# A two-stage attention kernel: the first slot of group 1 in an order of its own, three down-projections moved behind the slots of group 7

## The chip, the cores and the metric

The kernel runs on one NeuronCore of one Trainium2 chip. The metric is the device time of one launch in microseconds (us); less is better. A NeuronCore has engines that each take their own instructions in order: PE (TensorE, matrix products and transposes; PEld is its weight load), DVE (VectorE), ACT (ScalarE), POOL (GpSimd) and SP (SyncE, here the queue of most transfers). They meet through semaphores: an instruction waits until the instructions that it needs have counted up.

## What is computed

The reference has two stages. Stage one is a graph attention over 64 graphs of 64 nodes and 256 features; stage two is a transformer block with a conditioning vector per graph.

```python
# stage one: x is (64, 64, 256), q a vector per graph, adj a label array
self_feat = concat(x, q) @ W_self.T + b_self
output = self_feat
for d in range(2):                     # adjacency and its transpose
    cond, vb = A.sum(-1), A @ w_bias + b_bias
    aff = q_heads . k_heads * scale    # keys: the first 20 nodes alone
    w = softmax(where(cond > 0, aff, NEG) + vb)
    output += (w @ self_feat[:, :20]) @ Wout[d] + bout[d]
x = x + relu(output)
# stage two, per graph: shift, scale, gate from silu(time_emb) @ Wt + bt
h = layernorm(x) * (1 + scale_msa) + shift_msa
x = x + gate_msa * (attention(h) @ Wproj + bproj)     # 16 heads of 16
h = layernorm(x) * (1 + scale_mlp) + shift_mlp
x = x + gate_mlp * (gelu(h @ W1 + b1) @ W2 + b2)      # MLP of 1024
```

All of it is float32.

## The kernel before

**Groups and tiles.** The 64 graphs are cut into nine groups: 4 graphs, seven times 8, and 4 again. A tile (index j) is two graphs, 128 tokens; group 0 and group 8 have two tiles, the others four. Features lie on the partitions for the projections; the attention works on 128 tokens at a time.

**A software pipeline over groups, written out by hand.** The order of the program is the order on every engine's queue. `start()` does the graph stage of groups 0 and 1. Then, for g from 1 to 7, `boundary(g)` prepares projections, layer norms and masks, and `period(g)` runs the slots of group g. `finish()` ends groups 6 (its MLP), 7 and 8. In period(g) three things run side by side: the block attention of group g (E), the graph attention of group g+1 (C), and the MLP of group g-1. Each slot j takes one tile of each.

**A slot** (`slot`, L763) goes through these steps, and at named points (`fill("f0")`, `"f1"`, `"d0"`, ...) it inserts the work that a table in `period` (L976 to L1023) lists:

1. PE: scores of E and of C (L618, L458).
2. Transposes of the tile before, `block_turned(Eb)` (L654), copied to pT by ACT (L657). In the first slot of a period there is no tile before. Then f0.
3. POOL: masked keys for the next slot (L603, L441).
4. `block_exp(E)`: two maxima (L629) and two subtractions (L631) on DVE, an exponential on ACT (L635).
5. `graph_masked(C)`: two products on DVE (L469) and a sum on POOL (L474). Then f1.
6. `graph_turned` of the tile before (PE L496, ACT copies wT L500), if there is one.
7. `block_sums(E)`: a sum over keys on DVE (L639). Then d0.
8. `graph_exp(C)`: maximum (L479) and subtraction (L480) on DVE, exponential on ACT (L481). Then d0b.
9. `block_weights(E)`: a reciprocal on DVE (L642) and POOL's product (L643) that writes the normalised weights pr. The next slot's `block_turned` needs them.
10. Attention products of the tile before: pao (PE L665, ACT aoT L675), po (PE L514, DVE L523, ACT L524, POOL L525).
11. `graph_normal(C)`: sum and reciprocal on DVE (L486, L487), product on POOL (L488). Then d2 and f3.

**Fills that matter here.** `mlp_up` (L735) is a product on PE followed by a gelu on ACT (L737); `mlp_down(m, c, i)` (L745) adds block i of 8 to the output half c; a call of the 512-column form is two matmuls. `mlp_gated` (L680, DVE) reads the sum and gives its PSUM bank back, `mlp_out` adds on POOL (L758) and issues the output transfer on SP. `block_v` (L588) is a product on PE and four copies on ACT (L595). `self_cond` for group 3 is one product on POOL (L315) per half; `self_product` and `self_features` are pf on PE (L324) and an addition on DVE (L331). `half_normed` is the layer norm of the next group in four steps: transposes (L533), statistics (L542 to L546), normalising (L551), transposes back with scale and shift (L560, L563, L567). ACT has to load a table (ACT_TABLE_LOAD) between an exponential and a gelu; copies and biases need none.

**PSUM.** Most products take a bank from a ring of four (`free`); `mlp_down` holds one from its first block until `mlp_gated`, so that three go round. A product waits until the last reader of its bank is done.

**The two places.** In group 1's first slot the table puts `block_v(1, 1)` and the two `self_cond` of group 3 (`conds`) at f1, and four `mlp_up` at f3. In period 7, only three slots are run from the table, and the last tile's scores (E3) stand in `finish`; the table gives slot 2 `down(0, 2, 3)` at f0 and `down(0, 4, 5)` at f1, and `finish` goes on with 6 and 7:

```python
        E3 = block_scores(m, 3, [pair("pa", "sca"), pair("pb", "scb")])
        block_turned(before[0])
        half_normed(z, 2)
        mlp_down(l, 0, 6, 7)
        block_attended(before[0], bank("pao"))
        block_exp(E3)
```

Of the kernel before, what the change touches and what calls it, by code (L numbers as in the profile page):

```python
# [26 lines left out]
NG = len(NB)  # L27
# [19 lines left out]
def graph_attention_then_dit_block(  # L47
# [576 lines left out]
    def block_exp(t):  # L624
        mx = small.tile([P, 2, 2, 4], F32, tag="mx1", name="mx1")
        t.pr = two.tile([P, H, N], F32, tag="pr", name="pr")
        pa4 = [p_.rearrange("p q (h m) -> p q h m", m=N) for p_ in t.pa]
        for i in range(2):
            nc.vector.tensor_reduce(mx[:, i], pa4[i], AX.X, ALU.max)  # L629
        for i in range(2):  # L630
            nc.vector.tensor_tensor(  # L631
                t.pr[:, ts(i, 8)].rearrange("p (q h) m -> p q h m", q=2), pa4[i],
                mx[:, i].unsqueeze(3).to_broadcast([P, 2, 4, N]), ALU.subtract,
            )
        nc.scalar.activation(t.pr, t.pr, AF.Exp)  # L635

    def block_sums(t):
        t.sm = small.tile([P, H], F32, tag="sm1", name="sm1")
        nc.vector.tensor_reduce(t.sm, t.pr, AX.X, ALU.add)  # L639
# [5 lines left out]
    def block_normal(t):  # L645
        block_sums(t)
        block_weights(t)
# [91 lines left out]
    def mlp_down(g, c, *ms):  # L739
        G = groups[g]  # L740
        for m in ms:
            if m == 0:
                py, G.held = bank("py", hold=True)
                G.py = py[:, 0 : G.T]
            nc.tensor.matmul(G.py, w2_sb[:, m, ts(c, P)], G.u[m], start=(m == 0), stop=(m == 7))  # L745

    def mlp_gated(g, c):
        G = groups[g]
        if c == 0:
            y = gp.tile([P, 2, GT], F32, tag="h2T", name="y2T")  # L750
            G.y2T = [y[:, i, 0 : G.T] for i in range(2)]
        gated(G.y2T[c], G.py, "b2", 1, g, c)
        free.append(G.held)
# [6 lines left out]

    def slot(e, c, e_next, c_next, before, fill, late=False):  # L763
        Eb, Cb = before
        fill("p")
        sc = [pair("pa", "sca"), pair("pb", "scb")] if e or c else None
        E = block_scores(*e, sc) if e else None
        C = graph_scores(*c, sc) if c else None
        fill("p2")
        if Eb:  # L770
            block_turned(Eb)
        elif Cb:
            graph_turned(Cb[0])
        fill("f0")
        if e_next:
            block_keys(*e_next)
        if c_next and c_next[0] != 1:
            graph_keys(*c_next)
        if E:
            block_exp(E)  # L780
        if c_next and c_next[0] == 1:
            graph_keys(*c_next)
        if C:
            graph_masked(C)
        fill("f1")
        if Eb and Cb:
            graph_turned(Cb[0])
        if E:
            block_sums(E)
        fill("d0")  # L790
        if C and not late:
            graph_exp(C)
        fill("d0b")
        if E and not late:

            block_weights(E)
        if Eb:
            block_attended(Eb, pair("pa", "pao")[:, 0])
        fill("f2")
        for i, t in enumerate(Cb):  # L800
            if i > 0:
                graph_turned(t)
                fill("f2a")
            graph_output(t, pair("pa" if i > 0 else "pb", "po")[:, 0])
        if late:
            graph_exp(C)
            block_weights(E)
        fill("f2b")
        fill("d1")
        if C:  # L810
            graph_normal(C)
        fill("d2")
        fill("f3")
        return E, [C] if C else []
# [115 lines left out]
    def half_normed(g, step):  # L930

        G = groups[g]
        if step == 0:
            norm_tokens(G, G.xT, 0)
        elif step == 1:
            norm_stats(G)
        elif step == 2:
            normed(G)
        else:
            G.hT = new_hT("hT")  # L940
            modulated(G, G.hT, 0, amp1, off1, g)

    def run_slots(slots, fills, before):

        for i, (e, c) in enumerate(slots[: len(fills)]):

            def fill(where):
                for f, *args in fills[i].get(where, []):
                    f(*args)

            e_next, c_next = slots[i + 1] if i + 1 < len(slots) else (None, None)
            before = slot(e, c, e_next, c_next, before, fill, fills[i].get("late", False))
        return before

    def period(g):

        m, n, a = g - 1, g + 1, g + 2
        late = g + 2 >= NG

        def up(*ms):  # L960
            return [(mlp_up, m, i) for i in ms]

        def down(c, *ms):
            return [(mlp_down, m, c) + ms] if not late or c == 0 else []

        def masks(*steps):
            return [(mask_step, a, i) for i in steps] if a < NG else []

        def ahead(f, *args):
            return [(f, a) + args] if a < NG else []  # L970

        def next_(f, *args):
            return [(f, n) + args] if n < NG else []

        G = groups[g]
        gated_0 = [(mlp_gated, m, 0), (mlp_out, m, 0)]  # L976
        conds = ahead(self_cond, 0) + ahead(self_cond, 1)
        if G.nt == 2:
            fills = [
                {  # L980
                    "f0": up(0),
                    "f1": [(block_v, g, 0)] + up(1, 2),
                    "f3": up(3, 4, 5) + down(0, 0, 1, 2),
                },
                {
                    "f0": down(0, 3) + up(6),
                    "f1": up(7),
                    "f2": down(0, 4, 5),
                    "f3": down(0, 6, 7) + gated_0,
                },  # L990
            ]
        else:
            fills = [
                {
                    "f1": [(block_v, g, i) for i in range(1 if g in (1, NG - 2) else 0, 2)] + (conds if g == 1 else []),
                    "d0": masks(0) if g > 1 else [],
                    "d2": masks(1) + conds if g > 1 else [],
                    "f3": up(0, 1, 2, 3),
                },
                {  # L1000
                    "f0": down(0, 0, 1),
                    "f1": ahead(self_product, 0),
                    "d0": ahead(self_features, 0),
                    "f2b": ahead(self_product, 1),
                    "d1": ahead(self_features, 1),
                    "d2": masks(2, 3) if g > 1 else masks(0),
                    "f3": up(4, 5),
                },
                {
                    "f0": down(0, 2, 3),  # L1010
                    "f1": down(0, 4, 5),
                    "f2": ahead(graph_v, 0),
                    "d2": masks(3) if g == 1 else [],
                    "f3": up(6, 7),
                },
                {
                    "f0": next_(half_normed, 0) + down(0, 6),
                    "f1": down(0, 7) + gated_0 + next_(half_normed, 1),
                    "f2": down(1, 0, 1, 2),
                    "d0b": next_(half_normed, 2),  # L1020
                    "f3": down(1, 3, 4, 5, 6) + next_(half_normed, 3) + down(1, 7),
                },
            ]  # L1023
        if n == NG - 1:

            fills = fills[:3]
            fills[1].update(f0=down(0, 0), f2=down(0, 1))
            fills[2]["f3"] = up(6) + next_(half_normed, 0) + [(pair_proj, g, 0)] + up(7) + next_(half_normed, 1)
        C = groups[n].nt if n < NG else 0
        slots = [((g, j), (n, j) if j < C else None) for j in range(G.nt)]  # L1030
        return run_slots(slots, fills, (None, []))
# [117 lines left out]
    def finish(before):  # L1149

        z, m, l = NG - 1, NG - 2, NG - 3
        Z, A = groups[z], groups[m]
        K = [Tile() for _ in range(3)]
# [1 line left out]
        E3 = block_scores(m, 3, [pair("pa", "sca"), pair("pb", "scb")])  # L1155
        block_turned(before[0])
        half_normed(z, 2)
        mlp_down(l, 0, 6, 7)
        block_attended(before[0], bank("pao"))
        block_exp(E3)  # L1160
        mlp_gated(l, 0)
        mlp_out(l, 0)
        half_normed(z, 3)
        norm_tokens(K[0], A.xT, 0)
        mlp_down(l, 1, 0)
        block_normal(E3)
        norm_stats(K[0])
        mlp_down(l, 1, 1)
        mlp_down(l, 1, 2)
        block_qk(z, 1, 0)  # L1170
        block_qk(z, 1, 1)
        block_keys(z, 0)
        block_turned(E3)
        block_qk(z, 0, 0)
        block_qk(z, 0, 1)
# [70 lines left out]
    before = start()  # L1246
    for g in range(1, NG - 1):
        boundary(g, before)
        before = period(g)
# [60 lines left out]
```

## Time and profile before

| what | us |
|---|---|
| median of 3 runs | 675.4 (675.13 to 675.85) |
| the profiled execution | 675.26 |
| its span, first to last instruction | 673.6 |
| PE busy | 655.7 |
| DVE, ACT, POOL busy | 472.2, 354.9, 371.5 |
| granted TensorE clock | 1.00 throughout |

How to read the lines that follow. A line of a timeline has the start in us from the span's start, the duration in us, the engine, the line of the kernel, the operation, and output<-input by the names in the program, with the shape. Neighbouring instructions of the same kind are merged (x4), and their duration is from the first start to the last end. In brackets stands the engine's idle time just before, and what ended it. Matmuls are pipelined: ends are modelled, and a row's duration is longer than the distance to the next start. A line of the waits has the waiting engine, its operation, the engine and operation waited for, the total in us, the number of waits, and the longest. "The chain that ended last" is followed back from the last instruction, at each step to what released it.

### The profile page before, as it was taken

Reading aid. Unit: us, or ns where it says so; the run is one execution under the profiler, and the core shown is the slowest. Engines: PE = TensorE matmul, PEld = TensorE weight load, DVE = VectorE, ACT = ScalarE, POOL = GpSimd, SP = SyncE. Lnnn points to the kernel's source line nnn. Section 1 sums busy time; section 2 is a strip of 40 time slices with the busy share of each in tenths; the row PEclk is TensorE's granted clock in tenths of the full one; section 3 lists DMA queues with packets and bytes.
Section 4 is the critical chain, followed back from the end, with each engine's and each line's share of the span. In section 5 each row is a group of like instructions: output and inputs, shape, how many; then the busy total and the mean of one; then the engine's idle time right before and its main releaser. Section 6 shows DMA issues by size and latency. Waiting matters only on the chain.

```text
span 673.6 us, 15450 instructions
## 1 busy us (share of the span) xinstructions
PE 655.7 (97%) x6422; PEld 404.2 (60%) x6422; DVE 472.2 (70%) x859; ACT 354.9 (53%) x627; POOL 371.5 (55%) x366
## 2 busy tenths in 40 slices
PE   8999898999999999999999999999999999999997
PEld 7657656775555565565555655555565675556546
DVE  4988967997777677776776777776777865656221
ACT  3364537763666337744476436654377444854412
POOL 5556557756664567653584555744667546445210
PEclk9999999999999999999999999999999999999999
DMA  7626030014100310004000140003000000000000
GB/s 239 201 87 209 27 99 18 18 34 123 18 1 34 126 31 17 18 17 156 1 18 18 36 137 17 2 32 89 10 10 11 18 26 1 2 18 1 17 16 32
DMA packets 34654, 33.42 MB, mean 50 GB/s; under 512 B 5624, under 2 KB 28408, under 8 KB 34584
## 3 DMA queue, kind: packets, MB, share of 16 engines
q1 hardware_dynamic: 34104, 32.33, 15.2%
q8 instruction: 51, 0.84, 0.6%
q14 instruction: 19, 0.16, 0.1%
q10 hardware_dynamic: 416, 0.09, 0.1%
q0 software_dynamic: 64, 0.01, 0.0%
HBM read 25.59 MB, written 6.83 MB: 48 GB/s over the span
## 4 chain that ended last, share of the span: by engine, by line
PE 84%; DVE 7%; ACT 3%; POOL 2%; issue 1%; DMA 1%; SPq 0%; ACTq 0%; POOLq 0%; DVEq 0%
PE py L745 15%; PE pu L735 15%; PE pqT L422 8%; PE pqk L580 8%; PE ppT L654 4%; PE pv L588 4%; PE pwT L496 3%; PE pf L324 3%; PE pproj L690 3%; PE po L514 3%; PE pk L407 2%; PE pao L665 2%; PE pv L371 2%; PE sca L618 2%; PE pxT L533 2%; PE phT L560 2%
## 5 line engine op out<-in xcount | busy, mean ns | idle before, releaser
L745 PE MATMUL py<-u,w 128*128 128x512 f32 (+1 forms) x272 | 117.9, 561 | 0.2 <-ACT u L737 0.2
L735 PE MATMUL pu<-h2T,w 128*128 128x512 f32 (+1 forms) x256 | 108.8, 569 | 0.9 <-POOL h2T L567 0.5
L643 POOL TENSOR_TENSOR pr<-pr,sm 128x1024 f32<-128x1024 f32 x32 | 60.9, 1903 | 69.0 <-DVE sm L642 48.3
L474 POOL TENSOR_TENSOR w<-w,term 128x640 f32<-128x640 f32 x32 | 49.5, 1550 | 72.4 <-DVE w L469 39.4
L735 PEld LDWEIGHTS pu<-h2T,w 128*128 128x128 f32 x256 | 47.7, 190 | 48.6 <-issue 43.0
L745 PEld LDWEIGHTS py<-u,w 128*128 128x128 f32 x272 | 47.8, 190 | 36.4 <-issue 32.9
L737 ACT ACTIVATE u<-pu,vec 128x512 f32<-128x512 f32 (+1 forms) x72 | 43.2, 640 | 34.3 <-PE pu L735 34.1
L422 PE MATMUL pqT<-sfT,wq 128*128 128x512 f32 (+1 forms) x144 | 60.7, 551 | 0.3 <-DVE y L713 0.3
L580 PE MATMUL pqk<-hT,wqkv 128*128 128x512 f32 (+1 forms) x144 | 59.8, 551 | 0.5 <-POOL hT L567 0.4
L629 DVE TENSOR_REDUCE mx<-sca 128x8 f32<-128x512 f32 x32 | 22.0, 689 | 50.4 <-PE sca L458 49.0
L639 DVE TENSOR_REDUCE sm<-pr 128x16 f32<-128x1024 f32 x32 | 38.9, 1217 | 21.6 <-ACT pr L635 21.3
L481 ACT ACTIVATE w<-w 128x640 f32<-128x640 f32 x32 | 23.5, 736 | 57.9 <-DVE w L480 57.9
L423 ACT ACTIVATE qT<-pqT,vec 128x512 f32<-128x512 f32 (+1 forms) x36 | 23.0, 640 | 50.9 <-PE pqT L422 50.6
L635 ACT ACTIVATE pr<-pr 128x1024 f32<-128x1024 f32 x32 | 33.8, 1057 | 26.9 <-DVE pr L631 26.6
L657 ACT COPY pT<-ppT 128x512 f32<-128x512 f32 x64 | 34.4, 591 | 25.1 <-PE ppT L654 25.1
L546 POOL TENSOR_TENSOR rstd<-rstd,mhalf 128x2 f32<-128x2 f32 x32 | 23.3, 728 | 42.1 <-DVE rstd L545 41.1
L581 ACT ACTIVATE qk<-pqk,vec 128x512 f32<-128x512 f32 (+1 forms) x36 | 23.0, 640 | 43.4 <-PE pqk L580 43.4
L488 POOL TENSOR_TENSOR w<-w,sm 128x640 f32<-128x640 f32 x32 | 44.1, 1381 | 1.9 <-DVE sm L487 1.8
L551 DVE TENSOR_SCALAR xn<-xn,mv,rstd 128x256 f32<-128x256 f32 x64 | 37.9, 633 | 9.8 <-POOL rstd L546 9.8
L542 DVE BATCH_NORM_STATS2 st<-xn 128x6 f32<-128x256 f32 x64 | 26.1, 408 | 25.5 <-ACT xn L535 25.5
L525 POOL TENSOR_TENSOR xT<-xT,sfT 128x256 f32<-128x256 f32 x32 | 23.4, 731 | 32.6 <-ACT sfT L524 27.2
L500 ACT COPY wT<-pwT 80x512 f32<-80x512 f32 x64 | 34.0, 582 | 13.0 <-PE pwT L496 13.0
(146 smaller groups left out, 1429.7 us busy)
## 6 DMA issues: line engine op xcount, KB each, us to landing
xT<-in_x_t SPq DMA_DIRECT2D x7, 512.0 KB
out<-xT SPq DMA_DIRECT2D x14, 256.0 KB
a_d<-in_adj SPq DMA_DIRECT2D x7, 440.0 KB
a_d<-in_adj_t SPq DMA_DIRECT2D x7, 440.0 KB
x_g<-in_x SPq DMA_DIRECT2D x5, 512.0 KB
vblk<-vd SPq DMA_DIRECT2D x28, 80.0 KB
w<-in_w SPq DMA_DIRECT2D x2, 1024.0 KB
vd<-v_sb SPq DMA_DIRECT2D x7, 256.0 KB
```

Of the source, the lines that this page charges most:

```text
L422: nc.tensor.matmul(pq, wq_sb[d][:, k, ts(c, P)], G.sfT[:, k, :], start=(k == 0), stop=(k == 1))
L474: nc.gpsimd.tensor_tensor(t.w, t.w, G.term[:, :, j, :].unsqueeze(1).to_broadcast([P, H, 2, M]), ALU.add)
L488: nc.gpsimd.tensor_tensor(wf, wf, sm.unsqueeze(2).to_broadcast([P, 2 * H, M]), ALU.mult)
L500: nc.scalar.copy(t.wT[:, ts(q4, 4), :], pt[0 : 4 * M, :].rearrange("p (i t) -> p i t", i=4))
L551: nc.vector.tensor_scalar(key.xn[:, i, :], key.xn[:, i, :], key.mv[:, i, 0:1], key.rstd[:, i : i + 1], ALU.subtract, ALU.mult,)
L580: nc.tensor.matmul(pp, wqkv_sb[:, k, ds(i * D + c * P, P)], G.hT[:, k, 0 : G.T], start=(k == 0), stop=(k == 1))
L639: nc.vector.tensor_reduce(t.sm, t.pr, AX.X, ALU.add)
L643: nc.gpsimd.tensor_tensor(t.pr, t.pr, t.sm.unsqueeze(2).to_broadcast([P, H, N]), ALU.mult)
L657: nc.scalar.copy(t.pT[:, ts(q4, 4), :], pt.rearrange("p (i t) -> p i t", i=4))
L735: nc.tensor.matmul(pu, w1_sb[:, k, ts(m, P)], G.h2T[:, k, 0 : G.T], start=(k == 0), stop=(k == 1))
L737: nc.scalar.activation(G.u[m], pu, AF.Gelu, bias=col("b1", m))
L745: nc.tensor.matmul(G.py, w2_sb[:, m, ts(c, P)], G.u[m], start=(m == 0), stop=(m == 7))
```

## The change

In `slot`, a new flag `first` puts `block_weights(E)` directly behind `block_sums(E)`, ahead of d0 and of the graph's exponential. It is set for the first slot of group 1 only. The same slot gets a table of its own: `block_v(1, 1)` at f0, the four `mlp_up` at f1, `conds` at d0, nothing at d2 and f3.

In period 7, slot 2 keeps one down-projection (block 2), and blocks 3, 4 and 5 go to `finish`. There, 3 and 4 take the place of 6 and 7; 5, 6 and 7 follow behind the last tile's exponential and the last step of group 8's layer norm. `block_normal(E3)` (steps 7 and 9 of a slot) moves ahead of `mlp_gated` and `mlp_out`, `norm_stats(K[0])` moves ahead of the first block of the other half, and that half's blocks 1 and 2 move behind group 8's key projections.

```diff
-    def slot(e, c, e_next, c_next, before, fill, late=False):
+    def slot(e, c, e_next, c_next, before, fill, late=False, first=False):
...
         if E:
             block_sums(E)
+            if first:
+                block_weights(E)
         fill("d0")
         if C and not late:
             graph_exp(C)
         fill("d0b")
-        if E and not late:
+        if E and not (late or first):
...
-            before = slot(e, c, e_next, c_next, before, fill, fills[i].get("late", False))
+            before = slot(e, c, e_next, c_next, before, fill, *(fills[i].get(w, False) for w in ("late", "first")))
...
-                    "f1": [(block_v, g, i) for i in range(1 if g in (1, NG - 2) else 0, 2)] + (conds if g == 1 else []),
+                    "f1": [(block_v, g, i) for i in range(1 if g in (1, NG - 2) else 0, 2)],
...
+        if g == 1:
+            fills[0].update(first=True, f0=[(block_v, 1, 1)], f1=up(0, 1, 2, 3), d0=conds, d2=[], f3=[])
         if n == NG - 1:
 
             fills = fills[:3]
             fills[1].update(f0=down(0, 0), f2=down(0, 1))
+            fills[2].update(f0=down(0, 2), f1=[])
...
         half_normed(z, 2)
-        mlp_down(l, 0, 6, 7)
+        mlp_down(l, 0, 3, 4)
         block_attended(before[0], bank("pao"))
         block_exp(E3)
+        half_normed(z, 3)
+        mlp_down(l, 0, 5, 6, 7)
+        block_normal(E3)
         mlp_gated(l, 0)
         mlp_out(l, 0)
-        half_normed(z, 3)
         norm_tokens(K[0], A.xT, 0)
+        norm_stats(K[0])
         mlp_down(l, 1, 0)
-        block_normal(E3)
-        norm_stats(K[0])
-        mlp_down(l, 1, 1)
-        mlp_down(l, 1, 2)
         block_qk(z, 1, 0)
         block_qk(z, 1, 1)
         block_keys(z, 0)
+        mlp_down(l, 1, 1, 2)
         block_turned(E3)
```

## The prediction

> **What bounds the kernel now.** I read the page first (busy times, the chain that ended last), then the waits of PE (TensorE), then the timelines of every engine around the two places that the diff touches, and the chain inside the first of them.
>
> ```profile
> PE 655.7 (97%) x6422; PEld 404.2 (60%) x6422; DVE 472.2 (70%) x859; ACT 354.9 (53%) x627; POOL 371.5 (55%) x366
> ...
> PE 84%; DVE 7%; ACT 3%; POOL 2%; issue 1%; DMA 1%; SPq 0%; ACTq 0%; POOLq 0%; DVEq 0%
> ```
> and of the waits of PE the first line:
> ```profile
> PE ppT L654 <- POOL pr L643: 3.9, 3, 1.9
> ```
> PE is busy for 97% of the span and carries 84% of the chain. An edit that moves no matmul's cost can only change PE's idle time, about 18 us in all. The largest single cause is block_turned's transposes (L654) waiting for POOL's normalised weights (L643): 3.9 us in three waits. Two of these are where the diff works: 1.87 us in the second slot of group 1, and 1.10 us in the last stage. Between 121 and 547 us PE's timeline shows no gap over 0.14 us, so what the first place loses or wins stays to the end.
>
> First place, PE and then ACT, DVE and POOL:
> ```profile
> 107.71 1.13 PE L735 MATMUL pu<-h2T,w 128*128 128x256 f32 x4 [0.43 <-ACT v L595]
> 112.05 1.09 PE L654 MATMUL ppT<-ident,pr 128*128 128x128 f32 x8 [1.87 <-POOL pr L643]
> 118.24 1.98 PE L324 MATMUL pf<-xT,w_self 128*128 128x512 f32 x4 [0.45 <-DVE sfT L331]
> ...
> 106.15 1.50 ACT L595 COPY v<-pv 64x256 f32<-64x256 f32 x4
> 109.32 0.74 ACT L481 ACTIVATE w<-w 128x640 f32<-128x640 f32 x1 [1.67 <-DVE w L480]
> 110.08 1.28 ACT L737 ACT_TABLE_LOAD   x1
> 113.92 1.28 ACT L635 ACT_TABLE_LOAD   x1
> 115.22 1.06 ACT L635 ACTIVATE pr<-pr 128x1024 f32<-128x1024 f32 x1
> ...
> 116.31 1.22 DVE L639 TENSOR_REDUCE sm<-pr 128x16 f32<-128x1024 f32 x1 [1.88 <-ACT pr L635]
> 117.45 0.74 DVE L331 SCALAR_TENSOR_TENSOR sfT<-pf,vec,tq 128x512 f32<-128x512 f32 x1
> 110.09 1.90 POOL L643 TENSOR_TENSOR pr<-pr,sm 128x1024 f32<-128x1024 f32 x1
> ```
> The wait that comes last here is not the 1.87 us but the small one at 118.24. The chain inside this stretch runs from the scores (102.55) through the graph's exponential (109.32), the four gelus, the copies of pT and slot 1's exponential (115.22 on ACT) to L639, L331 and pf. The ppT wait is not on it: had ppT been ready earlier, PE would have stood before pf until 118.24 all the same.
>
> Second place (PE, POOL), and one more row of DVE and POOL from the start of the kernel:
> ```profile
> 592.02 0.72 PE L533 MATMUL pxT<-ident,xT 128*128 128x128 f32 x4
> 603.77 1.99 PE L580 MATMUL pqk<-hT,wqkv 128*128 128x256 f32 x8
> 606.87 1.09 PE L654 MATMUL ppT<-ident,pr 128*128 128x128 f32 x8 [1.10 <-POOL pr L643]
> 591.53 0.72 POOL L525 TENSOR_TENSOR xT<-xT,sfT 128x256 f32<-128x256 f32 x1
> ...
> 20.84 1.29 DVE L480 TENSOR_TENSOR w<-w,mx 128x640 f32<-128x640 f32 x1
> 22.90 0.82 DVE L480 TENSOR_TENSOR w<-w,mx 128x640 f32<-128x640 f32 x1
> 19.92 1.53 POOL L474 TENSOR_TENSOR w<-w,term 128x640 f32<-128x640 f32 x1
> ```
> The pxT group takes 0.72 us for four transposes that take 0.60 elsewhere: the third waits until 592.31 for POOL's L525, which ends at 592.25. So slot 2 of this period has no slack: PE arrives just when POOL is done.
>
> **Part 1: slot 0 of group 1.** PE's own order does not change: scores, block_v(1,1), four up-projections, before and after. What changes is the order on ACT, DVE and POOL.
>
> *ACT.* The four copies of v (1.50) now stand ahead of the exponential of E0. They wait for block_v's matmuls (102.69 + 1.99), so they run 104.72 to 106.22 and E0's exponential 106.23 to 107.29 instead of 105.07 to 106.13: 1.16 later. Behind it queue a table load (1.28), the gelus (1.57) to 110.17, another table load and the graph's exponential. The number of loads stays two. What the earlier copies give PE: the 0.43 wait for v goes.
>
> *DVE and POOL.* L639 107.32 to 108.54, L642 to 108.83, POOL's product L643 (1.90) 108.97 to 110.87, with the two tq products (2.66) now behind it. So ppT can start at 110.93, not 112.05: a gain of 1.12 there. L479 starts at 108.75 and L480 at 109.60; alone (0.82) it would end at 110.42. But L643 runs on POOL from 108.97. At 20.84 the same L480 beside a POOL product of the same kind took 1.29 and ended 0.68 after it (22.13 against 21.45); at 46.58 and 48.29 it again ended 0.68 after POOL's. With a block L480 ends at 110.87 + 0.68 = 111.55. Price between 0 and 1.13; I take 1.13, since three rows show it. The Trainium skill (SBUF — State Buffer, "SBUF: two separate sides") says that of a GpSimd operation and a DVE operation with two SBUF inputs, the later starter waits for the whole of the first; that would end it at 110.87 + 0.82 = 111.69, 0.14 later than the rows. I use the rows.
>
> *The exponential's table.* In every exponential L481 an event on ACT's queue waits for DVE, and at the first gelus (109.63, then 110.08) such events stand ahead of the load. So I let the load wait for L480: 111.68 to 112.96, exponential 112.98 to 113.72. If the load runs ahead, at 110.19, the exponential starts at 111.58. The skill (ScalarE: Activation LUTs, "What ACT_TABLE_LOAD costs") puts a switch at 2.66 us, load and drain; here ACT goes from load to activation in 0.01, and no drain is seen (110.08 + 1.28, then 111.37). With 2.66 the gelus end at 111.54 and the exponential starts at 114.36, 1.38 later still.
>
> *What is late next.* Behind that exponential on DVE stand L486 and L487, and slot 1's four steps of block_exp, since DVE takes its queue in order. Before, L486 started at 110.09 and the last L631 ended at 113.63, 3.54 later. Now: 113.75 + 3.54 = 117.29, slot 1's exponential at 117.32 instead of 115.22, thus +2.10. Its own table load (113.92) is gone from there, but DVE now sets the time. From that exponential to pf is 3.02 before (118.24 - 115.22): pf at 120.34, **+2.10 us**. PE's gains of 0.43 and 1.12 become waiting before pwT (L488 is late), po and pf. Bounds: +0.60 with neither block nor waiting load (exponential 111.48 to 112.22, slot 1's at 115.82), +3.5 with the skill's switch price; below zero only if pf did not depend on L331, and its row names L331.
>
> **Part 2: three down-projections.** Each is two matmuls at a spacing of 0.43, so 3 x 0.86 = 2.58 us of PE leave slot 2 (before 588.03) and enter the last stage.
>
> *Where they leave.* Slot 2's exponential on ACT (table load 585.61, exponential 586.90 to 587.96) depends on pT copies and DVE, not on the downs. L639, L642 and POOL's L643 (589.67 to 591.57) follow from it, then L525 to 592.25. None of that moves. PE would be 2.58 early: about 1.5 is lost before po (ACT's wT copies queue behind the exponential until 588.9, where pwT alone let them start at 588.67 before), the rest before the third pxT. Its start stays 592.31, so only its 0.07 of waiting is saved.
>
> *Where they enter.* Up to phT (600.07) nothing changes: two downs for two. Then three downs to 603.14, pxT to 603.58, one down to 604.44, the first k projection to 605.30. The second wants the bank that L680 empties; L680, now behind L639 and L642 (to 604.74) on DVE, ends at 605.40: a new wait of 0.16. Then two downs, and ppT at 608.15. The old waits vanish: 0.19 at 603.77 (due 603.58) and 1.27 at 606.87 (due 605.60 by spacing; the row's 1.10 counts from a modelled end). L643 is still 604.91 to 606.81 and no longer waited for. Sum: 2.58 - 0.19 - 1.27 + 0.16 = **+1.28**. On POOL, L758 with its output transfer and the statistics' power (L546) now stand behind L643: L546 ends near 608.7, xn at 610.1, and PE asks for it at 610.8; k's masks end by 609.9, asked for at 611.9. Later waits (0.60 at 616.43, 0.46 at 623.67) hang on PE's own work and stay. Bounds: -1.46 if slot 2 lost nothing, +2.58 if nothing is filled.
>
> **Sum.** 2.10 + 1.28 = 3.38 us. The profiled run took 675.26 with a span of 673.6; it becomes 678.6 with 677.0. On the median of 675.4 (0.1 above the profiled run): **678.8 us**.
>
> **Rivals.**
> *As laid out* (0.09): PE's waits for the product are the loss. The 0.43, 1.87 and 1.10 us go and nothing replaces them: 675.4 - 3.4 = 672.0. For it: they are the largest waits. Against: pf's wait for L331 and pxT's for L525 end later in the same slots. It decides for faster if slot 1's exponential starts before 115.22 and L525 ends before 591.0.
> *Mild loss* (0.13): block or waiting load does not fall on the chain. Load ahead: exponential at 111.58, slot 1's at 115.9, +0.7; no block but a waiting load: +0.97. Total 677.4 to 677.7.
> *One half comes free* (0.15): part 1 at zero because DVE's order is softer than I think, 676.7; or part 2's downs fill both waits and slot 2 does not stand still, 675.4 + 2.10 - 1.46 = 676.0.
> *More* (0.07): the late DVE and POOL of slot 1 also reach slot 2 of group 1, another 1 to 2 us, 680 to 681.
> That the change does nothing is part of it: PE's order in slot 0 is the same.
>
> **How the numbers follow.** The case as computed has 0.56 (678.3 to 679.4). With the mild loss, the half that comes free and the near part of "more" the range is 676.0 to 680.0. About 0.2% (1.35 us) is what a measurement of this kernel can tell from no change: slower 0.75, within 0.15, faster 0.10.
>
> **What would show it.** Right: ppT near 110.9 with a wait of 1.5 or less, slot 1's exponential near 117.3, L480 near 1.9 us long, pf near 120.3 with its wait grown; slot 2 near the end standing before po and pxT, ppT of the last tile without a wait. Wrong: L480 of 0.82 us, a pf wait below 0.5, or pxT's group starting its third transpose before 592.3 (plus part 1's shift).

## The result and the profile after

| kernel | median us | its profiled run | span of it |
|---|---|---|---|
| before | 675.41 (674.60 to 675.85, 6 runs) | 675.26 | 673.6 |
| after | 679.35 (677.66 to 679.94, 6 runs) | 679.33 | 677.6 |

The changed kernel takes 1.0052 times as long (95% interval 1.0038 to 1.0067), 3.9 us more. A repeat on another chip gave 678.67 against 674.87, 1.0053 (1.0036 to 1.0070).

The page of after: busy time of each engine, the granted clock of PE in 40 slices (tenths of full speed), and the chain that ended last.

```profile
PE 657.9 (97%) x6422; PEld 405.5 (60%) x6422; DVE 472.2 (70%) x859; ACT 354.9 (52%) x627; POOL 370.5 (55%) x366
...
PEclk9999899999999999999999999999999999999999
...
PE 82%; DVE 8%; ACT 3%; DMA 3%; POOL 2%; issue 1%; ACTq 0%; POOLq 0%; DVEq 0%
```

PE has the same 6422 instructions, but 2.2 us more busy time. The 8 in the fifth slice of the clock points to why. The longest PE waits of after:

```profile
PE pwT L496 <- POOL w L488: 2.5, 2, 1.8
PE ppT L654 <- POOL pr L643: 2.4, 2, 1.5
PE po L514 <- ACT wT L500: 2.2, 3, 1.4
```

The wait for pr fell from 3.9 to 2.4 us, as the change would have it, and two others of the same size stand in its place. Where they stand, in the first place (timelines of after: PE, ACT, DVE, POOL):

```profile
111.82 1.09 PE L654 MATMUL ppT<-ident,pr 128*128 128x128 f32 x8 [1.47 <-POOL pr L643]
117.26 1.07 PE L496 MATMUL pwT<-ident,w 128*80 128x128 f32 x8 [1.77 <-POOL w L488]
119.74 0.97 PE L514 MATMUL po<-wT,vblk 80*32 80x64 f32 x32 [0.51 <-ACT wT L500]
121.18 1.98 PE L324 MATMUL pf<-xT,w_self 128*128 128x512 f32 x4 [0.47 <-DVE sfT L331]
...
112.52 1.28 ACT L481 ACT_TABLE_LOAD   x1 [1.46 <-DVE w L480]
113.82 0.74 ACT L481 ACTIVATE w<-w 128x640 f32<-128x640 f32 x1
118.16 1.06 ACT L635 ACTIVATE pr<-pr 128x1024 f32<-128x1024 f32 x1 [2.65 <-DVE pr L631]
...
109.64 0.76 DVE L479 TENSOR_REDUCE mx<-w 128x32 f32<-128x640 f32 x1
110.43 2.01 DVE L480 TENSOR_TENSOR w<-w,mx 128x640 f32<-128x640 f32 x1
109.86 1.90 POOL L643 TENSOR_TENSOR pr<-pr,sm 128x1024 f32<-128x1024 f32 x1 [1.47 <-DVE sm L642]
```

Read from below: POOL's product ends at 111.76; L480, begun beside it, takes 2.01 us and ends at 112.44; the table load waits for L480; the exponential follows; slot 1's exponential (118.16) and pf (121.18) come out late. PE stands 1.47, then 1.77, 0.51 and 0.47 us.

The second place in after (PE, then POOL):

```profile
591.42 0.97 PE L514 MATMUL po<-wT,vblk 80*32 80x64 f32 x32 [1.40 <-ACT wT L500]
595.24 0.44 PE L533 MATMUL pxT<-ident,xT 128*128 128x128 f32 x2 [0.72 <-POOL xT L525]
610.99 1.04 PE L654 MATMUL ppT<-ident,pr 128*128 128x128 f32 x8
594.47 0.72 POOL L525 TENSOR_TENSOR xT<-xT,sfT 128x256 f32<-128x256 f32 x1
```

PE now stands 1.40 us before po and 0.72 before the third pxT transpose, and ppT of the last tile waits for nothing.

**One correction before positions are compared.** This profiled run had already lost time in code that the change does not touch. Windows of after around 78 us (stretch, its length, busy time of PE, PEld, DVE, ACT and POOL with instructions in brackets, granted clock, DMA share, GB/s):

```profile
76.40:79.80 3.40, 3.30 (x10) 2.44 (x11) 3.37 (x4) 1.17 (x2) 3.40 (x4) 0.50 0.09 19
```

For 3.4 us PE ran at half clock; before has 1.00 there. So the first C score of slot 0 is at 102.85 instead of 101.98, 0.87 us later. Distances from that score take this out; the repeat, whose run has no such stretch, has the score at 102.02.

| us from the first C score of slot 0 | before | predicted | after | repeat |
|---|---|---|---|---|
| E0's exponential | 3.09 | 4.25 | 4.27 | 4.27 |
| ppT of slot 1 | 10.07 | 8.95 | 8.97 | 8.97 |
| graph's exponential | 7.34 | 11.00 | 10.97 | 10.97 |
| slot 1's exponential | 13.24 | 15.34 | 15.31 | 15.31 |
| pf (second half) | 16.27 | 18.36 | 18.33 | 18.33 |
| from pf to the last tile's ppT | 488.62 | 489.90 | 489.81 | 489.80 |

### The profile page after: what moved, and what is told of

The parts are those of the page before. It is cut to its first block, busy times and chain, and to the rows that moved or that the text cites. A ratio compares the mean times of both kernels' runs of the same rounds, so it can differ in the third digit from the quotient of the medians.

```text
span 677.6 us, 15451 instructions
## 1 busy us (share of the span) xinstructions
PE 657.9 (97%) x6422; PEld 405.5 (60%) x6422; DVE 472.2 (70%) x859; ACT 354.9 (52%) x627; POOL 370.5 (55%) x366
## 3 DMA queue, kind: packets, MB, share of 16 engines
HBM read 25.59 MB, written 6.83 MB: 48 GB/s over the span
## 4 chain that ended last, share of the span: by engine, by line
PE 82%; DVE 8%; ACT 3%; DMA 3%; POOL 2%; issue 1%; ACTq 0%; POOLq 0%; DVEq 0%
PE py L745 15%; PE pu L735 14%; PE pqT L422 8%; PE pqk L580 7%; PE ppT L654 4%; PE pv L588 3%; PE pwT L496 3%; PE pf L324 3%; PE pproj L690 3%; PE po L514 2%; PE pk L407 2%; PE pv L371 2%; PE pao L665 2%; PE sca L618 2%; PE pxT L533 2%; PE phT L560 2%
## 5 line engine op out<-in xcount | busy, mean ns | idle before, releaser
L643 POOL TENSOR_TENSOR pr<-pr,sm 128x1024 f32<-128x1024 f32 x32 | 60.9, 1902 | 71.8 <-DVE sm L642 52.4
L639 DVE TENSOR_REDUCE sm<-pr 128x16 f32<-128x1024 f32 x32 | 38.9, 1217 | 21.7 <-ACT pr L635 21.4
L481 ACT ACTIVATE w<-w 128x640 f32<-128x640 f32 x32 | 23.5, 736 | 56.5 <-DVE w L480 55.5
```

Source lines behind the costliest of these rows:

```text
L643: nc.gpsimd.tensor_tensor(t.pr, t.pr, t.sm.unsqueeze(2).to_broadcast([P, H, N]), ALU.mult)
```

## The experiments

The changed kernel was run once more, and ten other kernels. A run counts as full clock when its mean granted clock is at least 0.9985. The baseline reached that in 38 of 75 runs of one chip (median 674.60); the other 37 had 0.997 (675.81). Times are medians in us; the ratio is against the kernel before on the same chip.

| kernel | median | ratio (95%) | full clock: runs, median |
|---|---|---|---|
| the change again | 678.67 | 1.0053 (1.0036 to 1.0070) | 3 of 6, 677.76 |
| part 1 alone | 678.04 | 1.0042 (1.0028 to 1.0057) | 3 of 6, 676.85 |
| part 2 alone | 676.41 | 1.0019 (1.0010 to 1.0028) | 12 of 21, 675.62 |
| L643 late again | 676.79 | 1.0030 (1.0020 to 1.0039) | 0 of 11 |
| L643 early, v late | 677.37 | 1.0032 (1.0020 to 1.0044) | 0 of 5 |
| part 1, v behind | 677.16 | 1.0030 (1.0020 to 1.0039) | 6 of 22, 675.38 |
| downs moved alone | 676.70 | 1.0016 (1.0006 to 1.0026) | 9 of 22, 675.64 |
| pf's input earlier | 675.38 | 1.0000 (0.9989 to 1.0011) | 10 of 22, 674.23 |
| wait filled | 674.77 | 0.9996 (0.9988 to 1.0003) | 20 of 21, 674.76 |
| both, ten products | 674.42 | 0.9989 (0.9981 to 0.9998) | 18 of 22, 674.34 |
| both, seven products | 674.13 | 0.9987 (0.9977 to 0.9997) | 17 of 21, 673.94 |

**The change once more**, unedited.

> The changed kernel once more, for more runs of it and their granted clocks. Theory (3.4 us of waits at full clock, and dips of the clock on top, since PE stands longer in the first place and before po and pxT): runs with clock 1.000 have a median of 677.9 to 678.2, against 674.6 for those of before; fewer than half of the runs keep clock 1.000; the median of all is near 679. Rival (dips are chance and as frequent as before): half of the runs at 1.000, median of all 678.6.

The steps came out the same to 0.02 us (table above). The times did not decide for the theory: 3 of the 6 runs have full clock, with a median of 677.76 (677.9 to 678.2 was expected), and the median of all is 678.67, close to the rival's 678.6. Six runs are too few to tell more.

**Part 1 alone**: the slot's edits, with period 7 and the finish as before.

> The first slot of group 1 in its new order, the last stage as before. Theory (the graph's exponential becomes late: L480 blocked beside POOL's L643, then a table load that waits for it): the distance from the first C scores of slot 0 to pf's second product grows by 2.1 us, from 16.26 to 18.3, and the time by about 2.1 us to 677.5 (ratio 1.003). Rival (PE's waits for the product and for v were the loss): the 1.87 and 0.43 us go, time 673.1, ratio 0.9966. Rival (the whole loss of the change comes from the last stage): no change, 675.4.

**Part 2 alone**: the slot as before.

```diff
+            fills[2].update(f0=down(0, 2), f1=[])
```

(and the changed finish.)

> The three down-projections moved and the new order of the last stage, the first slot of group 1 as before. Theory (slot 2 stands still for what it lost, since pxT waits for POOL's L525; the last stage fills 1.46 us of waits and gets one of 0.16): pxT's third transpose at an unchanged place, ppT of E3 1.2 to 1.3 us later, time 676.7, ratio 1.0019. Rival (the downs fill the wait of 1.1 us and cost nothing where they leave): 674.3, ratio 0.998.

At full clock part 1 alone is 676.85 - 674.70 (before on that chip) = 2.15 us slower, and part 2 alone 675.62 - 674.70 = 0.92. Together 3.07, near the 3.24 us of the distances (2.06 + 1.18). Both halves lose; no half came free.

**Is POOL's early product the blocker?** The slot of part 1, with L643 put back behind the graph's exponential and `conds` behind it:

```diff
-            fills[0].update(first=True, f0=[(block_v, 1, 1)], f1=up(0, 1, 2, 3), d0=conds, d2=[], f3=[])
+            fills[0].update(f0=[(block_v, 1, 1)], f1=up(0, 1, 2, 3), d0=[], d2=conds, f3=[])
```

> As p1_only, but block_weights stays behind graph_exp, and the tq products stand behind both: POOL's L643 no longer runs beside DVE's L480. Theory (the block is a part of the loss): L480 takes 0.82 us, the graph's exponential comes 1.4 us sooner than in p1_only, pf about 0.7 us later than before; time 676.1, ratio 1.001. Rival (the gelus' place and the table load alone make the loss, no block): as p1_only, 677.5. ppT should start near its old distance, since L643 starts late again: that this costs nothing is the test that ppT is not the bound.

Its DVE, ACT and PE timelines:

```profile
108.54 0.82 DVE L480 TENSOR_TENSOR w<-w,mx 128x640 f32<-128x640 f32 x1
115.07 1.06 ACT L635 ACTIVATE pr<-pr 128x1024 f32<-128x1024 f32 x1 [1.50 <-DVE pr L631]
111.62 1.33 PE L654 MATMUL ppT<-ident,pr 128*128 128x128 f32 x8 [2.93 <-POOL pr L643]
```

L480 is back at 0.82 us, and slot 1's exponential is 13.88 behind the first score: +0.64 on before, not +2.06. The table load now follows the gelus at once (gelus to 109.41, load at 109.44). So what is left is ACT's own new order: v copies, E0's exponential, load, gelus and a second load, all ahead of the graph's exponential. PE's wait for ppT, in turn, grew from 1.87 to 2.93 us. None of the 11 runs reached full clock, and the median is 0.7 us above the 676.1 expected. In the profiled run pf is 1.53 us later than before instead of 0.7, with a stretch at half clock from 112.33 to 115.75 ahead of it.

**Is it the product or the copies?** The product early, the v copies late, up-projections at f3:

```diff
+            fills[0].update(first=True, f1=[(block_v, 1, 1)], d0=conds, d2=[], f3=up(0, 1, 2, 3))
```

> Only block_weights ahead of graph_exp and the tq products behind it; block_v and the up-projections as before, so PE's and ACT's orders are those of before. Theory (the block): L480 starts beside L643 and takes about 1.9 to 2.0 us, the graph's exponential is 1.15 us later, and with it gelus, copies and slot 1's exponential; ppT's wait of 1.87 us goes, yet pf starts 1.1 us later; time 676.5, ratio 1.0017. Rival (ppT's wait is the loss): 673.5, ratio 0.9972.

In its DVE timeline L480 took 1.99 us and the graph's exponential came 1.17 later than before, as expected. One expectation failed. L643 ended at 108.68, and PE did not start ppT then (PE's timeline):

```profile
112.12 1.94 PE L654 MATMUL ppT<-ident,pr 128*128 128x128 f32 x8 [2.98 <-ACT u L737]
```

The wait is longer, and names another releaser: the gelus, which stand behind the graph's exponential on ACT and have yet to read the PSUM bank that ppT takes next. So ppT has two conditions, pr and a free bank; to make pr early is not enough. The kernel before has the second one nearly as late: there the first gelu ends at 111.85 (here 111.97), and ppT starts at 112.05, so that an earlier pr alone could have taken at most 0.2 of the 1.87 us. The 1.94 us of the row (1.09 elsewhere) are half clock. The time failed the expectation as well, 677.37 instead of 676.5: in the profiled run pf came 3.55 us later than before, not 1.1, behind the longer wait and 6.83 us at half clock. How much of it the order alone makes is not shown, since no run had full clock.

**The same, with the up-projections at f1 too**, so that against part 1 alone only block_v's place differs (period 7 and the finish are as before):

```diff
+            fills[0].update(first=True, f1=[(block_v, 1, 1)] + up(0, 1, 2, 3), d0=conds, d2=[], f3=[])
```

> As p1_only, but block_v(1,1) stays behind block_exp, so ACT's copies of v stand behind the first exponential as before; gelus still ahead of the graph's exponential, block_weights still first. Theory: the first exponential is at its old place, L643 starts 1.1 us sooner than in p1_only and L480, still blocked beside it, ends 1.1 us sooner; the table load then waits for the gelus; slot 1's exponential is 0.95 us later than before instead of 2.1, at full clock 675.6. Rival (the block and the table load make all of it, and the copies' place nothing): 676.8 as p1_only.

Its PE, ACT and DVE timelines:

```profile
110.88 1.09 PE L654 MATMUL ppT<-ident,pr 128*128 128x128 f32 x8
109.74 1.57 ACT L737 ACTIVATE u<-pu,vec 128x256 f32<-128x256 f32 x4
111.33 1.28 ACT L481 ACT_TABLE_LOAD   x1
109.18 1.99 DVE L480 TENSOR_TENSOR w<-w,mx 128x640 f32<-128x640 f32 x1
```

Slot 1's exponential is +0.97 on before and pf +0.97. L480 still takes 1.99 us, but here that is hidden: it ends at 111.17, and the load starts at 111.33, directly behind the last gelu (111.31). So the 0.97 is again ACT's order, not the block. With block_v at f0 as well, E0's exponential, the sum behind it and L643 come 1.18 later, and with them the end of the blocked L480; now the load waits for L480, and 0.97 becomes 2.06. The two do not add up, they need each other: with the gelus ahead, early copies without the block cost 0.64, the block without early copies is hidden (0.97), and together they cost 2.06. With the gelus behind the graph's exponential, as in the kernel before this one, nothing hid the block: that exponential came 1.17 later.

This version is also the nearest test of the largest wait. PE does not wait before ppT at all, which starts 8.13 us behind the first score instead of 10.07, and pf is 0.97 us later nevertheless.

**The moved down-projections alone**: period 7 as in part 2, the finish as before except that blocks 3 and 4 stand where 6 and 7 stood, and 5, 6, 7 directly behind `block_exp(E3)`.

```diff
-        mlp_down(l, 0, 6, 7)
+        mlp_down(l, 0, 3, 4)
         block_attended(before[0], bank("pao"))
         block_exp(E3)
+        mlp_down(l, 0, 5, 6, 7)
```

> The three down-projections moved, but the order of the last stage otherwise that of before (mlp_gated, half_normed, norm_tokens, block_normal as they stood); blocks 5, 6 and 7 directly behind the last exponential. It tells the move from the new order. Theory (slot 2 is bound by POOL's L525 and gives nothing for the work that leaves it): PE stands about 1.4 us before po and 0.7 us before pxT, ppT of E3 no longer waits and starts 1.0 to 1.1 us later counted from pxT's third transpose; at full clock 675.9. Rival (the loss of the last stage comes from its new order, L680 behind L639, not from the move): no later than before, 674.8 or less.

+1.04 at full clock, with the same 1.40 us before po. From the third pxT transpose to the last tile's ppT it is +1.04 as well, with ppT not waiting. With the rest of the new order (part 2 alone) that distance grows by 1.13 and the full-clock time by 0.92, so the rest is worth about 0.1 us either way: no difference that these runs can tell.

**Is the small wait before pf the one that counts?** On the kernel before, the first half's L331 is moved ahead of the sum L639 in slot 1 (its product pf stays where it was), so that the second half's pf need not wait for a late L331:

```diff
+        if g == 1:
+            fills[1].update(f1=ahead(self_product, 0) + ahead(self_features, 0), d0=[])
```

> The kernel before with one edit: in slot 1 of group 1 self_features of group 3, half 0 (DVE L331) stands ahead of block_sums (L639) instead of behind it. Theory (pf's second product is bound by L331, which waits behind slot 1's exponential, and ppT's wait is not the bound): the 0.45 us wait before pf goes, pf follows po directly, 0.6 us sooner; at full clock 674.2, ratio 0.999. Rival (pf is not bound by it, or L331 ahead of L639 makes the next step late): 674.8, no change.

```profile
113.17 1.41 PE L654 MATMUL ppT<-ident,pr 128*128 128x128 f32 x8 [1.87 <-POOL pr L643]
119.81 0.80 PE L514 MATMUL po<-wT,vblk 80*32 80x64 f32 x32
120.54 1.98 PE L324 MATMUL pf<-xT,w_self 128*128 128x512 f32 x4
```

In its PE timeline pf follows po at once, with the 1.87 us before ppT untouched. At full clock this gains 674.60 - 674.23 = 0.37 us (95% by resampling the full-clock runs: 0.2 to 0.8), of a wait of 0.45: the small wait was the binding one. In the median it gains nothing: 10 of its 22 runs have full clock, against 38 of 75, so the median falls among the runs below it. In the profiled run the clock fell at 113.79, within ppT.

**Does the 1.87 us wait cost clock?** On the kernel before, ten small products into a part of the score tile that nobody uses, between slot 1's scores and ppT. They leave nothing out.

```diff
+        if e == (1, 1):
+            for _ in range(10):
+                nc.tensor.matmul(sc[0][:, 1, 416:512], ident, ones[:, 0:96], start=True, stop=True)
```

> The kernel before with ten idle products of 96 columns (into a part of the score banks that nobody reads) in front of ppT in slot 1 of group 1, where PE waits 1.87 us; they add work that the reference does not have and leave none out. Theory (an idle stretch of PE of about 2 us there makes the chip grant half the clock for 3.4 us in about half of the runs, 0.9 us each): the granted clock is 1.000 in nearly all runs, the median falls to that of the runs before with clock 1.000, 674.8 against 675.2. Rival (the dips come from elsewhere, or from chance): the same share of runs with clock 0.997 as before, median 675.2 or later.

20 of 21 runs at full clock, against 38 of 75 without. The products hold ppT up a little (they took 2.47 us), so at full clock nothing is gained, 674.76 for 674.60; the median falls from 675.30 to 674.77, interval just across 1.

**Both together**, with ten products, then with seven.

> Both edits, sf_early and warm_fill, on the kernel before. Theory: their gains add, since one takes a wait away and the other a dip of the clock: 674.2 in nearly all runs with clock 1.000, ratio 0.9985, faster than both kernels. Rival: the products before ppT make ppT or DVE's maxima late (they share the score tile), and the gain of sf_early goes, 674.8.

> As sf_early_warm with seven idle products instead of ten: ten took 2.3 us at a spacing of 0.115 us and made ppT 0.36 us late; seven take 1.6 us and should end before POOL's product. Theory: ppT at its old distance (10.07 us from the first C scores), pf at 15.7 us instead of 16.07, nearly all runs at clock 1.000 with a median of 674.1, ratio 0.998 to 0.9985. Rival (0.3 us of idle time again lets the clock dip, or pf stays bound by wT behind the exponential): as sf_early_warm, 674.4, or half of the runs below clock 1.000.

PE of the version with seven (each product is two rows):

```profile
109.56 1.80 PE L772 MATMUL sca<-ones,ident 128*128 128x96 f32 x14
111.50 1.09 PE L654 MATMUL ppT<-ident,pr 128*128 128x128 f32 x8
116.46 0.80 PE L514 MATMUL po<-wT,vblk 80*32 80x64 f32 x32
117.19 1.98 PE L324 MATMUL pf<-xT,w_self 128*128 128x512 f32 x4
```

No wait before ppT, none before pf. Ten products had made ppT 0.36 us later than before; with seven it stands at 10.06 from the first C score, as before (10.07), and pf at 15.75 instead of 16.27. Both versions are a little faster than the kernel before, by intervals that end just below 1; the one with seven takes 674.13 against 675.36 (ratio 0.9987, 0.9977 to 0.9997).

## Why the prediction was right

678.8 was predicted, 679.35 measured, inside 676.0 to 680.0 and at the upper edge of the likeliest case (678.3 to 679.4). The steps came as computed, so the place in the range is not luck; the distance to 678.8 has a cause that the sum left out (below).

- **The v copies ahead of E0's exponential.** +1.16 predicted, +1.18 measured. The 0.43 wait for v went and came back as waiting, as said.
- **L480 blocked.** Begun beside L643 and ending 0.68 us after it (112.44 against 111.76), the value taken from three rows, not the full 0.82. L643 late again, with L480 at 0.82, confirms the cause. The reduction L479 before it, with one input, overlapped the same product by 0.54 us, and neither was held up (0.76 and 1.90).
- **The load waits for L480.** 1.46 us in its row, named so. The price of the switch was the row's 1.28, not the 2.66 that the prediction weighed and set aside. With block and waiting load gone (L643 late again), slot 1's exponential was +0.64, near the predicted lower bound of +0.60.
- **pf.** +2.10 predicted, +2.06 measured. The term in between, 3.02 from slot 1's exponential to pf, stayed (18.33 - 15.31).
- **ppT earlier by 1.12, of no use.** Measured 1.10; the waits moved to pwT, po and pf. One sign was badly chosen: "a pf wait below 0.5" was to show the prediction wrong, and "its wait grown" to show it right. The wait before pf is 0.47 us, 0.02 more than before, though pf is 2.06 later: the standing spread over the waits ahead of it.
- **Slot 2 of period 7.** The distance from pf to the third pxT transpose is 474.06 before and after: 2.58 us less work, and not 0.01 us sooner. "About 1.5" before po is 1.40.
- **The last stage.** +1.28 predicted, +1.18 measured; the new wait on L680's bank was 0.17. The last hundredths are spacing between matmuls.

**The rivals.** "As laid out" fell: ppT's wait did shrink, and pf was late all the same. "Mild loss" fell with the 2.01 us of L480 and the 1.46 us of the load. "One half comes free" fell with the halves alone. "More" did not happen: from pf to pxT nothing was added.

**The term that was missing.** The prediction's sum took the clock as 1.00, and said that the edit can only change PE's idle time. The places give 2.06 + 1.18 = 3.24 us at full clock, and full-clock runs agree: 677.76 (5 of 12 runs of the change) - 674.60 = 3.16. The medians differ by 3.9 and 3.8 us. The rest, some 0.6, goes with stretches at half clock, which both kernels have. That the changed kernel has them in more of its runs is not shown (7 of 12, against 37 of 75). But when it has them they are longer or more: of those 7 runs 4 have a mean clock of 0.994, which part 2's trace shows with two stretches, while the 37 of the baseline have 0.997, one stretch. They are at 678.9 to 680.5, the baseline's near 675.8. So the forecast of +3.4 on the median was 0.1 to 0.2 too high for the work, and left out about 0.6 for the clock. Which wait brings on a given stretch in the changed kernel is argued, not shown: no version of it with its waits filled was run.

## What to carry to other kernels

Follow each wait to the one that binds last in the same stretch before moving work for the largest one: here the 1.87 us could be taken away with pf later, not earlier, while 0.45 us beside it were worth 0.37 at full clock. What the large wait did cost was clock: with it filled, the median fell by 0.5 us (interval just across 1). Work taken out of a slot that another engine paces does not make it shorter; it is paid again where it goes. Before an elementwise POOL product is moved forward, look at which DVE operation with two SBUF inputs will start beside it, and who waits for that. And before making an input early, look for a second condition, here the PSUM bank.

## What the runs showed of the hardware

- **PE's clock falls after waits that look harmless.** Eight of the thirteen traces have stretches at clock 0.50, twelve in all; each lasts 3.41 us, or twice that (6.83). One made what follows 0.87 us late in after, and runs below full clock are 1.2 us longer in the baseline (675.81 - 674.60). Most begin within or shortly behind waits of 0.9 to 3 us. The kernel before has one wait of 1.87 us in an otherwise full stretch, and lost clock in 37 of 75 runs; with that wait filled by ten products, in 1 of 21 (with pf's input earlier as well, in 4 of 22, and with seven products in 4 of 21). With waits of 2.93 and 2.98 us there, in all 16. The Trainium skill (TensorE: Matmul & The Clock Gate, "Why this matters for your kernels") sets the mark at idle gaps of over some 3 us; half of the runs here lost clock below it. Windows of the kernel with L643 early and v late, columns as above:

```profile
105.00:111.00 6.00, 3.71 (x74) 2.51 (x72) 4.94 (x5) 3.10 (x7) 5.71 (x4) 1.00 0.00 0
111.00:119.00 8.00, 6.88 (x20) 4.69 (x21) 4.88 (x10) 5.57 (x9) 5.38 (x6) 0.57 0.01 2
119.00:125.00 6.00, 6.00 (x114) 4.15 (x112) 4.78 (x9) 4.75 (x9) 3.37 (x5) 1.00 0.00 1
```

  PE is idle for over 2 of 6 us, then runs at a clock of 0.57 on average, then full again: the price comes after the wait, mostly in products that themselves wait for nothing.
- **The clock changes in steps of 3.41 us.** In part 2's trace it falls at 111.89 and at 589.75, 477.86 us apart, which is 140 steps of 3.413; in every trace, the distances between its changes are whole multiples of that. Whether a given wait falls into one step or across two therefore differs from trace to trace. But this does not decide alone: the 1.40 us before po lay within one step in after and in part 2's trace, and the clock fell behind it in the second only. Why the same wait costs clock in one run and not in another stays open.
- **A load of ACT's table did not run ahead of an unready activation.** Where L481 waited for DVE, its load waited too (1.46 us in after), although ACT had nothing else to do.
